# Reordering TensorE's instruction stream at the last and at the first pair of chunks: four handed-over matmuls, and four quadrant matmuls

## The chip, the cores and the metric

The kernel runs on one core of a Trainium2 chip. The metric is the device time of one execution in microseconds, given as the median of three runs.

## The reference: what is computed

The input x has 1024 examples, each with 64 features of 16 elements. Three layers of a compressed interaction network follow. Each forms all products of a feature of x with a feature of the layer's own input, and maps them by a weight matrix:

```python
z = jnp.einsum('bfe,bge->bfge', x0, h)          # all products of two features
y = jnp.einsum('oc,bce->boe', Ws[i], z) + bs[i][None, :, None]
if split_half and i != n - 1:
    x_i, h = (y[:, :half, :], y[:, half:, :])   # half to the output, half to the next layer
...
pooled = jnp.sum(jnp.concatenate(xs, axis=1), axis=2)
return pooled @ fc_w.T + fc_b
```

Everything is in float32; the output is one number for each example.

## The kernel before, in words

**Chunks and tiles.** The batch is cut into 32 chunks of 32 examples, so that a chunk has 32 x 16 = 512 columns. The pairs of features are laid out as 16 tiles (4 groups j of 4 tiles i) of 128 rows. A product block `z` holds one group: 128 x 4 x 512. VectorE makes most blocks (`w_product`, line 633; `product`, line 241), GpSimd some. 14 blocks exist, and each goes back to a list when its last reader has been written (`take`, `used`).

**What TensorE accumulates.** Since the last layer is followed only by a sum and a dot product, the kernel folds its weights: from each chunk it needs a hidden layer (`w_all[..., 0:64]`, 64 rows) and a second linear map of the same products, called q (`w_all[..., 64:128]`, 64 rows). Their elementwise product, summed, together with a term from x (`x_v0x`, line 289), gives the output. Every matmul of this part writes 64 output rows, thus one half of the array's columns; the code alternates between an upper and a lower half of a bank, so that two matmuls can stand in the array together.

**Pairs.** From chunk 6 on, chunks are taken two at a time, a and b, in 13 pairs. Two chunks times two maps are a 2 x 2 block product, and a scheme of seven instead of eight products is used. Its names: X, T2, T3, T4, B21, B22 are blocks and their sums and differences; alpha, beta, gamma, delta are accumulators in PSUM (`alpha` and `gamma` are the two row halves of one bank, `delta` and `beta` halves of two others). GpSimd makes the sums and differences (`w_mix`, line 650). One of them, the second group of T4 = T2 + B21, is made by an accumulating DMA that GpSimd issues (`nc.gpsimd.dma_start(..., accum_op=ALU.add)`, line 648).

**Order.** Nothing is scheduled automatically: `at(when, ...)` notes an operation with a place number, `zipped` notes two columns of matmuls that interleave, and all operations are then sorted by that number and issued. Per pair, `window` puts out two columns of matmuls: X with wq, T2 with s2, T3 with s1 to alpha in the first column; T3 with s3 and T2 with the hidden weights to delta, and T-blocks to beta, in the second. Four of the delta matmuls, those that read the T4 block made by DMA (`p4_run(p)[-LATE:]`), are left out there and handed over to the next pair's window, where they stand in the two `fill` lists (`first_fill`, `second_fill`); the eight B22 matmuls go there too (`late_run`). All matmuls of this part share line 525.

**Quadrant matmuls.** `squares` (placed at t + 30.2 in each window) issues four 64 x 64 matmuls that add squares of x and form y; they take one quadrant of the array each. VectorE's end-of-pair operations follow (`end_pair`): `w_hb` (line 671), `w_qa` (line 675), `w_uu` for alpha (line 681), `w_ha` (line 678), `w_uu` for delta (line 681), `x_v0x` (line 289), `sums` (line 293).

**The end.** The 13th pair has no window after it. Its handed-over work is zipped with the q matmuls of chunks 2 and 3 (`end_q`, first 384 columns, then 128), whose hidden layer is known from the start. `end_squares` issues their four quadrant matmuls and ends in line 929 and two ScalarE copies (931); `end_gamma` adds gamma to alpha (ScalarE 941, VectorE 942). `add_parts` (950), `end_uu` (935), pooling matmuls and output DMAs close the kernel.

Of the kernel before, what the change touches and what calls it, by code (L numbers as in the profile page):

```python
# [50 lines left out]
NI = 4  # L51
NJ = 4
NT = NI * NJ
# [11 lines left out]
GROUPS = [(j, i) for j in range(2) for i in range(NI)]  # L65
LATE = 4
# [3 lines left out]
def cin_kernel(ctx, tc, xra, xrb, wh, w0r, w1h, w2t, wx1, wx0, vec, out):  # L70
# [297 lines left out]
    for h in range(2):  # L368
        at = slice(32 * h, 32 * h + 32)
# [145 lines left out]
    def at(when, fn, *args, **flags):  # L515
        ops.append((when, len(ops), fn, args, flags))

    def zipped(when, *columns):
        for n, column in enumerate(columns):
            for m, job in enumerate(column):  # L520
                if job is not None:
                    at(when + m + n / len(columns), *job)
# [37 lines left out]
    def q_extra(c, w, out=None):  # L560
        out = accs[c][halves[1 - c % 2]] if out is None else out[halves[c % 2]]
        mm(out, w, es[c])
# [59 lines left out]
    def w_run(p, out, w, name, start=False, at_t=0, order=GROUPS):  # L622
        return [
            (w_job, p, out, w, j * NI + i + at_t, name, start and n == 0)
            for n, (j, i) in enumerate(order)
        ]
# [58 lines left out]
    def make_pair(t, p, when, mixed):  # L685
        a, b = p["a"], p["b"]
        for when, c, j, name, uses in (
            (when[0], b, 2, "B22", 5), (when[1], b, 0, None, 0), (when[2], b, 0, "T3", 9),
            (when[3], a, 0, "X", 5), (when[4], b, 3, "B22", 5), (when[5], b, 1, None, 0),
            (when[6], b, 1, "T3", 9), (when[7], a, 1, "X", 13 if p["k"] > 3 else 5), (when[8], a, 2, "B21", 5),  # L690
            (when[9], a, 3, "B21", 5),
        ):
            if name is None:
                at(t + when, w_both, p, j)
                continue
            if name == "B21" and j == 2 and p["k"] == 3:
                at(t + when, w_product, p, c, j, name, uses, engine=nc.gpsimd)
                continue
            if name != "T3":
                ahead = 3.3 if p["k"] > 4 and name == "B22" and j == 2 else 2.7  # L700
                if p["k"] == 3 and name == "X" and j == 1:
                    ahead = 9.1
                at(t + when - ahead, second, c, j)
            at(t + when, w_product, p, c, j, name, uses)
        t2, t1, t4 = ("T2", "X", "T3"), ("T3", "B22", "T2"), ("T2", "T2", "B21")
        for when, j, names in zip(
            mixed, (0, 1, 1, 0, 1, 1, 0), (t2, (*t2, 0, 2), (*t2, 2), t1, t1, t4, t4)
        ):
            at(t + when, w_mix, p, j, *names)
        at(t + 29, lambda: used(p["B21"][1]))  # L710

    def p4_run(p):
        return w_run(p, delta, wh_all, "T2", at_t=2 * NI)

    def first_fill(p):
        return [(lambda: q_extra(p["a"], va, p["beta"]),)] + p4_run(p)[-LATE : -LATE // 2]

    def second_fill(p):
        return p4_run(p)[-LATE // 2 :]

    def late_run(p, out=alpha, first=0, last=2 * NI):
        jobs = w_run(p, out, s4, "B22", out is gamma)[first:last]
        return jobs if last < 2 * NI else jobs + [(lambda: q_extra(p["b"], vb, p["alpha"]),)]
# [5 lines left out]
        v0x(b, "set")  # L729
        v0x(a, "set")  # L730

    def window(t, p, fill, late, pad=[], order=GROUPS[NI:] + GROUPS[:NI]):
        zipped(
            t,
            w_run(p, alpha, wq_all, "X", True, order=order) + fill[0] + w_run(p, alpha, s2, "T2")
            + fill[1] + w_run(p, alpha, s1, "T3"),
            w_run(p, delta, s3, "T3", True) + late + w_run(p, beta, wq_all, "B21", True, 2 * NI)
            + pad + p4_run(p)[:-LATE],
        )
        at(t + 30.2, squares, p)  # L740
        at(t + 7.3, snap_p1, p)
        at(t + 7.8, snap_p7, p)
        at(t + 7.3 + len(fill[0]) + 8, snap_u2, p)

    def end_pair(t, p, whens):
        hb_, qa, uub, ha, uua, xv, add = whens
        at(t + hb_, w_hb, p)
        at(t + qa, w_qa, p)
        at(t + uub, w_uu, p, alpha, "A", snaps[2])
        at(t + ha, w_ha, p)  # L750
        at(t + uua, w_uu, p, delta, "O", snaps[0])
        at(t + xv, x_v0x, p["k"])
        at(t + add, sums, p["k"])


    def load_pair(t, p, b0, a0, b1, a1):
        a, b = p["a"], p["b"]
        at(t + b0, load_xa, b)
        at(t + b0, load_xb, b, 2, 0)
        at(t + a0, load_xa, a)  # L760
        at(t + a0, load_xb, a, 0)
        at(t + b1, load_xb, b, 3, 1)
        at(t + a1, load_xb, a, 1, 2, 3)
        for c in (b, a):
            at(t + 1, load_e, c)
            at(t + 14, square, c)
        at(t + 1.1, load_xx, p["k"])
# [65 lines left out]
    for n in range(NPAIR):  # L833
        k = n + 3
        s = k % 2
        p = {
            "k": k, "A": halves[s], "O": halves[1 - s], "b": 2 * k + s, "a": 2 * k + 1 - s,
        }
        pairs.append(p)
        t = T0 + SPAN * n  # L840
        if n == 0:
            load_pair(t, p, -39.9, -33.3, -33.15, -27)
            make_pair(
                t, p, (-23.4, -20.7, -20.4, -17.8, -17.2, -16.8, -16.6, -7, -13.5, 3),
                (-14, -6.9, -6.8, 7.2, 12.4, 17.6, 17.5),
            )
            left5 = [[(contract_half, 5, 3, i, n) for i in (2, 3)] for n in range(2)]
            window(
                t, p, ([left5[1][0], (q_extra, 4, va)], [left5[1][1]]),
                [left5[0][0], (q_extra, 5, va), None, None], [left5[0][1], None],  # L850
                GROUPS,
            )
        else:
            q = pairs[-2]
            load_pair(t, p, -34, -28, -27.8, -27.7)
            make_pair(
                t, p, (-21.4, -18.7, -18.4, -15.8, -12.2, -9.5, -6.1, -2, 1.6, 4.2),
                (-5, 1.6, 3.6, 7.2, 12.4, 18.6, 18.5),
            )
            window(t, p, (first_fill(q), second_fill(q)), late_run(q))  # L860
            end_pair(t, q, (0.7, 11.7, 17.9, 22.3, 23.2, 24, 27.5))
# [40 lines left out]
    t, q = T0 + SPAN * NPAIR, pairs[-1]  # L902
# [64 lines left out]
        plain_product(t + when, c, j)  # L967
    for when, c in ((-5, 2), (0, 3)):
        at(t + when, product, c, NJ - 1, engine=nc.gpsimd, uses=NI)
    end_pair(t, q, (0.7, 4.5, 13.8, 8.5, 9, 9.5, 14.5))  # L970
    at(t + 10.5, end_gamma)
    at(t - 0.1, new_ends)
    zipped(
        t,
        first_fill(q) + second_fill(q) + late_run(q, gamma, 0, 2)
        + [(end_q, 3, m, 0) for m in range(NT)] + [(end_extra, 3, 0)],
        [(end_q, 2, m, 0) for m in range(3)] + late_run(q, first=2)
        + [(end_q, 2, m, 0) for m in range(3, NT)] + [(end_extra, 2, 0)],
    )
# [102 lines left out]
```

## Time and profile before

| | |
|---|---|
| median of 3 runs | 458.56 us (457.4 to 459.05) |
| the profiled execution | 458.11 us, of which the span from first to last instruction is 456.3 us |
| mean granted TensorE clock | 0.996 |
| TensorE matmul busy | 447.7 us (98%) |
| VectorE busy | 392.8 us (86%) |
| GpSimd busy | 364.4 us (80%) |
| ScalarE busy | 116.5 us (26%) |
| a 64-row, 512-column matmul record | 0.593 us mean, started 0.43 us apart |
| accumulating DMA z<-z, 1 MB, 13 of them | 8.6 / 9.5 / 12.3 us from issue to landing (least, median, longest) |

PE is TensorE's matmuls, PEld its weight loads, DVE VectorE, ACT ScalarE, POOL GpSimd, SP the engine on whose queue the loads from memory are issued. "A <-B" behind an idle time says what ended the wait. Times in the timeline count from the span's start. A matmul's record includes filling and draining, so that neighbours overlap: its cost is read from the distance of starts. One matmul of the code stands as two records.

### The profile page before, as it was taken

To read this page: it belongs to the slowest core of one execution; us is meant where nothing else is said; L and a number is where in the kernel's file an instruction comes from. 1 tells how busy PE (TensorE), PEld (TensorE's weight loads), DVE (VectorE), ACT (ScalarE), POOL (GpSimd) and SP (SyncE) were. 2 spreads that over 40 slices of the span, in tenths; PEclk is the share of its full clock that TensorE was granted. 3 is DMA by queue.
4 is the path that set the end of the run, shared out by engine and by line. 5 is a ranking of instruction groups with operands and counts; after the bars stand their busy time and mean duration, and the time that the engine had idled before them with its cause. 6 is when DMAs were issued, how large, how long until landed. Compare 5 with 4: busy or idle time off the path is not lost.

```text
span 456.3 us, 6069 instructions
## 1 busy us (share of the span) xinstructions
PE 447.7 (98%) x2302; PEld 161.6 (35%) x2302; DVE 392.8 (86%) x284; ACT 116.5 (26%) x215; POOL 364.4 (80%) x125
## 2 busy tenths in 40 slices
PE   8999999999999999999999999999999999999897
PEld 4565343332333333333333333333333333333235
DVE  4995499998989998989999998999999899998443
ACT  3162251232313113121312312231321313133011
POOL 5423688998997979799897979899797979979700
PEclk9999999999999999999999999999999999999899
DMA  8996998496839396784939587593949769571400
GB/s 304 408 306 151 315 407 338 138 317 194 286 82 344 106 268 228 172 323 103 354 87 293 190 208 290 117 381 65 312 149 253 256 136 386 111 232 23 105 0 2
DMA packets 34484, 99.67 MB, mean 218 GB/s; under 512 B 6324, under 2 KB 6996, under 8 KB 27864
## 3 DMA queue, kind: packets, MB, share of 16 engines
q1 hardware_dynamic: 31800, 84.70, 51.7%
q0 software_dynamic: 1872, 13.63, 16.6%
q10 hardware_dynamic: 784, 0.95, 0.8%
q8 instruction: 18, 0.29, 0.3%
q14 instruction: 10, 0.08, 0.0%
HBM read 84.00 MB, written 1.64 MB: 188 GB/s over the span
## 4 chain that ended last, share of the span: by engine, by line
PE 80%; DVE 10%; issue 4%; DMA 4%; POOL 1%; SPq 0%; ACT 0%; POOLq 0%; ACTq 0%
PE alpha L525 48%; PE delta L525 9%; PE acc L525 6%; PE acc L251 6%; DVE z L633 5%; PE q L525 3%; PE acc L269 3%; PE beta L525 3%; DMA z<-z 2%; DMA z<-in_w0r 2%; DVE acc L293 1%; POOL z L650 1%; DVE uu L289 1%; DVE uu L681 1%; DVE delta L678 1%
## 5 line engine op out<-in xcount | busy, mean ns | idle before, releaser
L650 POOL TENSOR_TENSOR z<-z,z 128x2048 f32<-128x2048 f32 (+1 forms) x78 | 299.8, 3876 | 29.6 <-PE alpha L525 29.6
L633 DVE TENSOR_TENSOR z<-xa,xp 128x2048 f32<-128x2048 f32 x103 | 231.6, 2279 | 1.2
L525 PE MATMUL alpha<-z,ws 128*64 128x512 f32 x624 | 219.5, 593 | 0.0
L525 PEld LDWEIGHTS alpha<-z,ws 128*64 128x64 f32 x624 | 69.4, 137 | 117.6 <-issue 117.6
L525 PE MATMUL delta<-z,w_all 128*64 128x512 f32 x208 | 97.2, 601 | 3.4 <-DMA z<-z 2.3
L553 ACT COPY xp<-xb 128x512 f32<-128x512 f32 x88 | 51.5, 587 | 167.0 <-DVE z L633 140.6
L525 PE MATMUL alpha<-z,w_all 128*64 128x512 f32 x208 | 92.0, 595 | 0.8
L525 PE MATMUL delta<-z,ws 128*64 128x512 f32 x208 | 92.0, 595 | 0.0
L525 PE MATMUL beta<-z,w_all 128*64 128x512 f32 x208 | 91.7, 593 | 0.0
L241 DVE TENSOR_TENSOR z<-xa,xp 128x2048 f32<-128x2048 f32 (+2 forms) x23 | 45.1, 2001 | 6.8 <-ACT xp L553 5.8
L525 PEld LDWEIGHTS alpha<-z,w_all 128*64 128x64 f32 x208 | 27.5, 137 | 63.6 <-issue 53.0
L241 POOL TENSOR_TENSOR z<-xa,xb 128x2048 f32<-128x2048 f32 x6 | 27.5, 4644 | 20.5 <-DMA xb<-in_xrb 20.5
L525 PEld LDWEIGHTS delta<-z,w_all 128*64 128x64 f32 x208 | 28.7, 139 | 36.0 <-issue 30.3
L251 PE MATMUL acc<-z,w_all 128*64 128x256 f32 x256 | 29.0, 382 | 1.1 <-DVE z L241 0.9
L525 PE MATMUL acc<-z,w_all 128*64 128x512 f32 (+1 forms) x96 | 29.4, 594 | 0.0
L525 PEld LDWEIGHTS beta<-z,w_all 128*64 128x64 f32 x208 | 27.9, 137 | 0.0
L525 PEld LDWEIGHTS delta<-z,ws 128*64 128x64 f32 x208 | 27.5, 137 | 0.1
L664 ACT ACTIVATE snap<-alpha,vs 64x512 f32<-64x512 f32 x13 | 8.9, 682 | 54.3 <-PE alpha L525 54.3
L251 PEld LDWEIGHTS acc<-z,w_all 128*64 128x64 f32 x256 | 18.0, 137 | 13.3 <-DVE z L241 2.5
L661 ACT COPY snap<-alpha 64x512 f32<-64x512 f32 x13 | 7.6, 581 | 48.8 <-PE delta L525 48.8
L293 DVE TENSOR_REDUCE acc<-uu 128x64 f32<-128x1024 f32 (+2 forms) x19 | 19.6, 1036 | 0.2
L681 DVE SCALAR_TENSOR_TENSOR uu<-alpha,snap 64x512 f32<-64x512 f32 x13 | 9.0, 689 | 12.1 <-PE alpha L525 12.1
(117 smaller groups left out, 361.1 us busy)
## 6 DMA issues: line engine op xcount, KB each, us to landing
xa<-in_xra SPq DMA_DIRECT2D x32, 1024.0 KB, 9.7
xb<-in_xrb SPq DMA_DIRECT2D x128, 256.0 KB, 7.8
z<-z POOLq DMA_DIRECT2D x13, 1024.0 KB, 9.5
e<-in_xra SPq DMA_DIRECT2D x28, 128.0 KB, 6.8
xx<-in_xra SPq DMA_DIRECT2D x28, 128.0 KB, 5.7
z<-in_w2t SPq DMA_DIRECT2D x2, 1024.0 KB
z<-in_wx SPq DMA_DIRECT2D x2, 1024.0 KB, 9.4
z<-in_w1h SPq DMA_DIRECT2D x1, 1024.0 KB
```

Of the source, the lines that this page charges most:

```text
L241: engine.tensor_tensor(blocks[zs[c, j]][:, at, :], xas[c][:, at, :], xbs[c][j].unsqueeze(1).to_broadcast([128, last - first, N]), ALU.mult,)
L251: nc.tensor.matmul(accs[c][halves[n]], w_all[:, t, 0:64], blocks[zs[c, j]][:, i, n * H2 : (n + 1) * H2], start=(t == 0), stop=(j == last a ...
L269: nc.tensor.matmul(accs[c][halves[1 - c % 2]], w_all[:, t, 64:128], blocks[zs[c, j]][:, i, :], start=(t == 0), stop=False, skip_group_chec ...
L289: nc.vector.scalar_tensor_tensor(uu[:, to, :], ys[k], cx, xxs[k], ALU.add, ALU.mult)
L293: nc.vector.tensor_reduce(acc[rows, of, k, half], uu[rows, of if at is None else at, E * half.start : E * half.stop].rearrange("p k (b e) ...
L525: nc.tensor.matmul(out, w, rhs, start=start, stop=stop, skip_group_check=True)
L553: nc.scalar.copy(bank, xbs[c][j])
L633: engine.tensor_tensor(blocks[b], xas[c], xbs[c][j].unsqueeze(1).to_broadcast([128, NI, N]), ALU.mult)
L650: nc.gpsimd.tensor_tensor(*(blocks[b][:, first:last] for b in (o, x, y)), ALU.subtract if in1 == "T3" else ALU.add,)
L661: nc.scalar.copy(snaps[0][p["O"]], alpha(p))
L664: nc.scalar.activation(snaps[1][p["O"]], alpha(p), AF.Identity, bias=bh1[p["A"]])
L681: nc.vector.scalar_tensor_tensor(uu[p[out], 0], x(p), 1.0 / QS, factor[p[out]], ALU.mult, ALU.mult)
```

## The change

In the last pair the four handed-over delta matmuls, which stood right after the beta matmul in the first column, are put behind gamma's two matmuls and the first six q matmuls of chunk 3. VectorE's `w_ha` and its `w_uu` go from places 8.5 and 9 to 13.3 and 13.5. In the first pair's window `squares` goes from t + 30.2 to t + 21.9, ahead of the last T3 matmul of group 0, the four of group 1, and the four delta matmuls that interleave with those.

```diff
-    def window(t, p, fill, late, pad=[], order=GROUPS[NI:] + GROUPS[:NI]):
+    def window(t, p, fill, late, pad=[], order=GROUPS[NI:] + GROUPS[:NI], quads=30.2):
...
-        at(t + 30.2, squares, p)
+        at(t + quads, squares, p)
...
                 [left5[0][0], (q_extra, 5, va), None, None], [left5[0][1], None],
-                GROUPS,
+                GROUPS, 21.9,
...
-    end_pair(t, q, (0.7, 4.5, 13.8, 8.5, 9, 9.5, 14.5))
+    end_pair(t, q, (0.7, 4.5, 13.8, 13.3, 13.5, 9.5, 14.5))
...
     zipped(
         t,
-        first_fill(q) + second_fill(q) + late_run(q, gamma, 0, 2)
-        + [(end_q, 3, m, 0) for m in range(NT)] + [(end_extra, 3, 0)],
+        first_fill(q)[:1] + late_run(q, gamma, 0, 2) + [(end_q, 3, m, 0) for m in range(6)]
+        + p4_run(q)[-LATE:] + [(end_q, 3, m, 0) for m in range(6, NT)] + [(end_extra, 3, 0)],
         [(end_q, 2, m, 0) for m in range(3)] + late_run(q, first=2)
         + [(end_q, 2, m, 0) for m in range(3, NT)] + [(end_extra, 2, 0)],
     )
```

The second column is as before. The order on GpSimd and on SP's queue is the same in both kernels.

## The prediction

> **What bounds the kernel now.** The page comes first: engine shares and slices.
>
> ```profile
> PE 447.7 (98%) x2302; PEld 161.6 (35%) x2302; DVE 392.8 (86%) x284; ACT 116.5 (26%) x215; POOL 364.4 (80%) x125
> PE   8999999999999999999999999999999999999897
> PEclk9999999999999999999999999999999999999899
> ```
>
> TensorE is busy nearly everywhere; so only a place where it stands idle, or runs slowly, has time to give. The slices show one: PE and its clock dip to 8 in slice 38 (from 422 us). The chain in order of time says what ends there.
>
> ```profile
> 416.50 0.50 POOL z L650
> 417.08 1.14 issue
> 418.26 1.87 issue
> 420.13 9.17 DMA z<-z
> 429.34 0.91 PE delta L525
> ...
> 438.49 0.57 PE hx L525
> 439.51 11.14 PE q L525 x90
> ```
>
> The chain leaves TensorE for an accumulating DMA (z<-z, issued on POOL's queue at L648) and comes back at 429.34. From there to the end it is TensorE again. The timeline of that place (start, duration, instruction, idle before it):
>
> ```profile
> 429.34 1.11 PE L525 MATMUL delta<-z,w_all 128*64 128x512 f32 x1 [2.27 <-DMA z<-z]
> 430.24 1.06 PE L525 MATMUL delta<-z,w_all 128*64 128x512 f32 x1
> 431.10 1.06 PE L525 MATMUL delta<-z,w_all 128*64 128x512 f32 x1
> ...
> 432.74 0.59 PE L525 MATMUL delta<-z,w_all 128*64 128x512 f32 x1
> 433.17 0.59 PE L525 MATMUL delta<-z,w_all 128*64 128x512 f32 x1
> ```
>
> Read the starts: 0.86 to 0.90 apart at first, 0.43 later. Each matmul of the code stands in the trace as two records, so one 512-column matmul costs 0.86 us warm and 1.7 in this slow stretch; one of 384 columns costs 0.64 (records 0.32 apart). Stage windows (last columns: granted clock, DMA share, GB/s) confirm it:
>
> ```profile
> 427.00:432.70 5.70, 3.43 (x10) 1.65 (x11) 0.68 (x1) 0.00 (x0) 3.05 (x1) 0.70 0.05 15
> 432.70:438.40 5.70, 5.70 (x29) 2.03 (x25) 2.03 (x3) 0.00 (x0) 0.00 (x0) 1.00 0.00 0
> ```
>
> The first pair's end, from the timeline, has the change's other place:
>
> ```profile
> 107.06 0.64 PE L525 MATMUL delta<-z,w_all 128*64 128x512 f32 x1 [1.11 <-POOL z L650]
> 110.64 0.64 PE L525 MATMUL alpha<-e,vs 64*64 64x512 f32 x1
> 111.66 0.64 PE L525 MATMUL alpha<-z,w_all 128*64 128x512 f32 x1
> 111.75 0.76 DVE L671 SCALAR_TENSOR_TENSOR snap<-alpha,vs,snap 64x512 f32<-64x512 f32 x1 [1.84 <-PE y L525]
> 119.31 0.13 PEld L525 LDWEIGHTS delta<-z,w_all 128*64 128x64 f32 x1 [0.59 <-DMA z<-z]
> 119.43 0.59 PE L525 MATMUL delta<-z,w_all 128*64 128x512 f32 x1
> ```
>
> TensorE idles 1.11 for POOL's last difference; the quadrant matmuls (64x64) stand behind it, 1.02 us with their drains. The line to remember is 119.31: the next pair's handed-over matmuls need that pair's DMA, and their weight load already waits 0.59 for it. The DMA was issued at 106.92 and took 12.3 us, the longest of the 13 (median 9.5); DMA share there is about 1.
>
> **What the Trainium skill says.** "TensorE: Matmul & The Clock Gate", Part 1: an idle TensorE falls to half clock, judged over free-running windows of about 3.4 us. The trace agrees: half speed after an idle of 2.27, none after 1.11. Where between these the threshold lies depends, by that page, on the window's phase. "TensorEngine Tiling (Array Packing)", Key Properties: tiles execute independently; a change of tiling mode drains the array. The trace agrees: an alpha matmul begins at 431.96, ahead of a delta (432.74) that precedes it in program order but goes to the other column half; and there is about 0.1 us at each side of quadrant matmuls.
>
> **Part 1, the last pair.** Removed: nothing. Moved: four delta matmuls from steps 1 to 4 of the first column to steps 9 to 12, behind two gamma and six of chunk 3's q. POOL's and SP's orders stay, so DMA issue times do too.
> Gone: the idle from about 426.9, when the next matmul could have begun, to 429.34 (2.44), and the slow stretch: four deltas took 429.34 to 434.46, 5.12 instead of 4 x 0.86 = 3.43, so 1.69. By 432.5, when the new order reaches delta, the DMA has been there for three microseconds; the first column has had beta, two gammas and six q, 0.86 + 1.72 + 3.86, since 426.0.
> Added: the order counts by column half, since the two run side by side. Up to the quadrants: the second half has 3 q (1.93) and 7 of 512 columns (6.02), 7.95; the first now has 7.30. Gamma's first matmul is now at step 1 and carries a wait on DVE in the built order: it overwrites a part of alpha's bank that L671 has just read. L671 runs from 426.08 to 426.84, and beta occupies the array to 426.9; I charge 0.25 for wait and restart, with the second q behind it. Quadrants at 426.0 + 7.95 + 0.25 + 0.1 = 434.3, done at 435.35 (1.02). After them the first half has 3 deltas (2.58) and 11 q (7.08) and sets the pace: 445.0. In the trace before the 384-column q end at 448.5. **Sum: -3.5.** If the halves went in lockstep, each mixed step at 0.86, it would be 0.5 less (13 x 0.86 + 11 x 0.64 against 17.0 by columns, less what the second half already holds): -3.0.
> DVE: L678 and its L681 move behind L289, L929 and L942. Nothing waits for them but the sums. Had they stayed, L289 would stand behind the late delta, and the second y bank's reuse with it. Chain: delta's last at about 438.2, L942 ends at 438.8 (hx 435.4, L929 0.7, three ACT copies 1.8, L942 0.7), then L678 0.7, two L681 1.4, sums 1.2, L289 0.75, sums 0.7, L950 0.7: 444.4, ahead of the 445.2 at which L935 wants DVE. Cover: 0.8 us; beyond that the end is late one for one.
> After 445 the 128-column q, pooling and output follow unchanged.
>
> **Part 2, the first pair.** The quadrants go between the third and fourth T3 matmul of the first half, 104.9. Third ends at 104.92, quadrants to 106.04, fourth to 106.9: all in front of POOL's end at 106.99. The four differences then start at 107.06 as before, and the next pair at 110.55 instead of 111.66: 1.11 gained. Its DVE input ends at 109.91, in time; L671 loses its 1.84 wait, so DVE runs 1.8 early. But the next thing is the DMA: the delta behind beta is reached at 118.3 instead of 119.4, its data land at 119.31. TensorE stops for 1.0 and goes on at 119.43, as before. **Sum: 0.** Idle time moves from 106 to 118. Worse is possible: DVE's early products release SP's next chunk load at about 115.3 instead of 117.05, and it competes with the accumulation for its last 2 us. Accumulating beside little other traffic took 9.2 us, in contention 12.3; so up to 2 x (1 - 9.2/12.3) = 0.5 is lost. I take +0.1.
> The later pairs keep their rhythm of 26.1 to 26.3 us, since every long wait in them (POOL and ACT on alpha, DVE on alpha) is on TensorE. Their accumulations have slack: 131.86 + 9.5 = 141.4, used at about 145.5.
>
> **Sum against the profile.** The profiled execution took 458.11 (span 456.3), 0.45 below the median of 458.56; the change is a difference, so -3.4 from the median: **455.1**.
>
> **Rivals.**
> *Part 2's gain is kept.* If the accumulation came about 1 us sooner, the 1.0 would be carried to the end: -4.5, 454.1. For: later pairs saw 9.5 us. Against: neither its issue nor its traffic moves to the better. Chance 0.10.
> *It lands later, or the new stop at 118.3 cools the clock.* A stop of 1.5 lies between 1.11 (stayed warm) and 2.27 (did not). Up to 0.5, and 1.7 more if cold: 455.6 to 457.3. Chance 0.16.
> *DVE's tail.* If L678's chain is over 0.8 late, L935 and the pools wait; losing 1 to 2: 456 to 457. For: delta is its last input. Against: the sum above. Chance 0.07.
> *Slower: unequal matmuls don't run side by side.* The place is the first-column steps with a q against a 512-column matmul, 12 now where there were 6. Were each pair serial (1.50), the stretch takes 12 x 1.50 + 0.86 + 11 x 0.64 + 1.1 = 27.0 from 426.0: 453.0, 4.5 later than before: 463. It turns slower once a mixed step costs about 0.3 above 0.86. Against: at 436 to 438 q and alpha records overlap at 0.32 and 0.43. Chance 0.04.
> *The change doesn't do what it says.* The built order has the matmuls where the diff puts them, with their waits; only a cold clock at the end for another reason would leave 457. Chance 0.03.
>
> **How the numbers follow.** My forecast (0.60) has 454.7 to 455.6. The range 453.8 to 456.9 takes in the kept gain, the later landing and most of DVE's tail. About 0.5%, 2.3 us, is what a measurement of this kernel can tell from no change, so faster means below 456.3: the forecast, the kept gain, and most of the late landings, 0.84; same 0.12 (cold clock, tail, no effect); slower 0.04.
>
> **What would show it.** Right: no DMA wait of PE between 424 and 446; clock 1.00 there; the first gamma at 426.9; L678 behind L942. In the first pair: no gap ahead of the quadrants at 105, next pair at 110.5, and a new PE wait on DMA z<-z of about 1 us at 118.3. Wrong: no such wait (the gain was kept), q records 0.43 apart beside alpha, or L935 held by DVE's own queue.

## The result, and the profile after

Over seven runs each, the kernel after took 453.6 us in the median (453.13 to 454.65), the kernel before 458.16 (455.37 to 459.05): a ratio of 0.991, 95% interval 0.9886 to 0.9935. The forecast was 455.1, with a range from 453.8; the median lies 0.2 below its low end. The forecast was counted from the 458.56 of three runs; on that scale the ratio of 0.991 gives 454.4. The profiled execution took 453.26 us, span 451.4, clock 1.000, against 458.11, 456.3 and 0.996.

The page of the kernel after, engine shares and slices:

```profile
PE 446.7 (99%) x2302; PEld 162.4 (36%) x2302; DVE 392.8 (87%) x284; ACT 116.6 (26%) x215; POOL 364.7 (81%) x125
PE   8999999999999999999999999999999999999997
```

The dip in slice 38 is gone. The chain in order of time (start, length, what) of the same kernel no longer goes through a DMA at the end:

```profile
423.60 0.57 PE alpha L525
424.62 0.47 PE beta L525
426.96 0.43 PE alpha L525 x2
431.25 0.43 PE delta L525
431.69 0.43 PE delta L525
432.11 0.86 PE alpha L525 x3
432.97 0.57 PE hx L525
433.99 0.47 PE delta L525
436.71 9.06 PE q L525 x76
```

From beta to the last q matmuls it is TensorE alone. The timeline of the last pair on TensorE (start, duration, instruction, idle before it in brackets where there is one):

```profile
424.55 0.64 PE L525 MATMUL beta<-e,va 128*64 128x512 f32 x1
425.03 0.59 PE L525 MATMUL beta<-e,va 128*64 128x512 f32 x1
425.46 0.64 PE L525 MATMUL alpha<-z,ws 128*64 128x512 f32 x1
...
431.09 0.59 PE L525 MATMUL delta<-z,w_all 128*64 128x512 f32 x1
431.52 0.59 PE L525 MATMUL delta<-z,w_all 128*64 128x512 f32 x1
...
432.91 0.64 PE L525 MATMUL y<-e,v 64*64 64x512 f32 x1
...
433.92 0.64 PE L525 MATMUL delta<-z,w_all 128*64 128x512 f32 x1
...
443.64 2.13 PE L525 MATMUL q<-z,w_all 128*64 128x128 f32 x32
```

No bracket, and 0.43 us from start to start. The stage windows (length, then busy time of PE, PEld, DVE, ACT, POOL, then clock, DMA share, GB/s) confirm full clock in the 11 us in which the kernel before idled and ran slowly:

```profile
426.70:432.40 5.70, 5.70 (x31) 2.87 (x27) 0.30 (x1) 0.00 (x0) 1.95 (x1) 1.00 0.01 3
432.40:438.10 5.70, 5.70 (x34) 2.45 (x34) 2.06 (x3) 1.81 (x3) 0.00 (x0) 1.00 0.00 0
```

From beta's start to the start of the first 128-column q that follows the last 384-column one it takes 443.64 - 424.55 = 19.09 us; before, 448.52 - 425.99 = 22.53. So the last pair gave 3.44 of the 4.9 by which the spans differ.

The other 1.44 is the earlier start of beta, and the first pair shows where it comes from. TensorE and its weight loads in the kernel after:

```profile
103.75 1.02 PE L525 MATMUL alpha<-z,ws 128*64 128x512 f32 x2
104.70 0.64 PE L525 MATMUL alpha<-e,vs 64*64 64x512 f32 x1
...
105.72 0.64 PE L525 MATMUL alpha<-z,ws 128*64 128x512 f32 x1
105.72 0.64 PE L525 MATMUL delta<-z,w_all 128*64 128x512 f32 x1
...
109.21 0.59 PE L525 MATMUL alpha<-z,w_all 128*64 128x512 f32 x1
...
110.06 0.59 PE L525 MATMUL delta<-z,ws 128*64 128x512 f32 x1
```

```profile
117.94 0.13 PEld L525 LDWEIGHTS delta<-z,w_all 128*64 128x64 f32 x1 [0.88 <-DMA z<-z]
```

The quadrants stand where the prediction put them, the wait for GpSimd is gone, and the weight load of the handed-over delta now waits 0.88 for the accumulating DMA. But that DMA was issued earlier than before. GpSimd's timeline, first of the kernel after, then of the kernel before:

```profile
69.04 4.56 POOL L536 TENSOR_TENSOR z<-z,vs 128x2048 f32<-128x2048 f32 x1 [1.65 <-DMA z<-in_wx]
105.50 0.98 POOL L648 DMA_DIRECT2D z<-z  x1
```

```profile
70.67 9.13 POOL L536 TENSOR_TENSOR z<-z,vs 128x2048 f32<-128x2048 f32 x2 [2.47 <-DMA z<-in_wx]
106.92 0.96 POOL L648 DMA_DIRECT2D z<-z  x1
```

GpSimd's chain begins with the landing of two weight blocks (`in_wx`, L536) and then runs without a long wait to L648. In this execution it started 1.63 earlier there, at a place where the two programs are the same, and reached L648 1.42 earlier. The experiments ask whether this belongs to the change.

### The profile page after: what moved, and what is told of

The parts are those of the page before. It is cut to its first block, busy times and chain, and to the rows that moved or that the text cites. A ratio compares the mean times of both kernels' runs of the same rounds, so it can differ in the third digit from the quotient of the medians.

```text
span 451.4 us, 6068 instructions
## 1 busy us (share of the span) xinstructions
PE 446.7 (99%) x2302; PEld 162.4 (36%) x2302; DVE 392.8 (87%) x284; ACT 116.6 (26%) x215; POOL 364.7 (81%) x125
## 4 chain that ended last, share of the span: by engine, by line
PE 84%; DVE 10%; issue 3%; DMA 1%; SPq 0%; ACT 0%; ACTq 0%
PE alpha L525 51%; PE delta L525 10%; PE acc L525 7%; PE acc L251 6%; DVE z L633 5%; PE q L525 3%; PE acc L269 3%; PE beta L525 3%; DMA z<-in_w0r 1%; DVE acc L293 1%; DVE uu L289 1%; DVE uu L681 1%; DVE delta L678 1%; DVE xp L639 1%; PE y L525 0%
## 5 line engine op out<-in xcount | busy, mean ns | idle before, releaser
L650 POOL TENSOR_TENSOR z<-z,z 128x2048 f32<-128x2048 f32 (+1 forms) x78 | 300.0, 3881 | 29.5 <-PE alpha L525 29.3
L525 PE MATMUL delta<-z,w_all 128*64 128x512 f32 x208 | 95.8, 593 | 0.0
L525 PE MATMUL q<-z,w_all 128*64 128x384 f32 (+1 forms) x128 | 20.0, 382 | 0.0
```

Source lines behind the costliest of these rows:

```text
L525: nc.tensor.matmul(out, w, rhs, start=start, stop=stop, skip_group_check=True)
L650: nc.gpsimd.tensor_tensor(*(blocks[b][:, first:last] for b in (o, x, y)), ALU.subtract if in1 == "T3" else ALU.add,)
```

## The experiments

Theory A: the last pair gives all, and the first pair nothing, since the accumulating DMA lands some 12.4 us after its issue and TensorE meets it. Rival B: the first pair's gain is kept, and with it the other 1.4 us. Rival C: the moved quadrants make the DMA land later, or cool the clock. All the runs with this DMA in its place can be set side by side once GpSimd's arrival is taken out: the table's last column is the profiled execution's time less the issue of the first pair's L648.

| kernel | ratio to before, interval | profiled time | L648 issued | beta starts | beta less L648 | beta to 128-column q | time less L648 |
|---|---|---|---|---|---|---|---|
| before | | 458.11 | 106.92 | 425.99 | 319.07 | 22.5 | 351.2 |
| before, again | 1.0015, 0.9995 to 1.0034 | 457.78 | 106.48 | 425.63 | 319.15 | 22.5 | 351.3 |
| first pair only | 1.0001, 0.9979 to 1.0022 | 456.54 | 106.89 | 425.87 | 318.98 | 21.1 | 349.7 |
| last pair only | 0.9928, 0.9903 to 0.9953 | 454.30 | 106.54 | 425.61 | 319.07 | 19.1 | 347.8 |
| after | 0.991, 0.9886 to 0.9935 | 453.26 | 105.50 | 424.55 | 319.05 | 19.1 | 347.8 |
| after, again | 0.9924, 0.9901 to 0.9947 | 454.13 | 106.51 | 425.52 | 319.01 | 19.1 | 347.6 |
| after, third | 0.9933, 0.9913 to 0.9954 | 454.36 | 106.77 | 425.67 | 318.90 | 19.1 | 347.6 |
| gamma only | 0.9952, 0.9935 to 0.9969 | 455.86 | 107.66 | 426.72 | 319.06 | 19.6 | 348.2 |

**The kernel before once more** (no edit), on one chip with the three that follow:

> The kernel before, unchanged, for a second trace. Theory A (GpSimd's arrival): how early the first pair's accumulating DMA is issued varies between executions with the landing of the in_wx loads, so its issue lies anywhere between 105 and 107 us, and the delta matmul of the next pair starts 12.4 us after the issue or at its own reach of about 118.3 to 119.4, whichever is later. Rival B (the change moves it): the kernel before always issues it at about 106.9, and 119.4 follows. Ratio 1.000 for both; the last pair's idle of 2.0 to 2.5 us before the first delta and slow matmuls behind it.

Measured: 458.02 us, ratio 1.0015 (0.9995 to 1.0034). The trace has the same stop for the DMA, 2.23 us, and from about a microsecond behind it the records stand 0.86 apart. L648 was issued at 106.48, and the next pair's delta waited for its landing at 119.02, which is theory A's picture. Over all comparisons the runs of this one program reach from 455.35 to 459.73: 4 us, as much as the change is worth.

**The first pair alone:**

```diff
-    def window(t, p, fill, late, pad=[], order=GROUPS[NI:] + GROUPS[:NI]):
+    def window(t, p, fill, late, pad=[], order=GROUPS[NI:] + GROUPS[:NI], quads=30.2):
...
-        at(t + 30.2, squares, p)
+        at(t + quads, squares, p)
...
-                GROUPS,
+                GROUPS, 21.9,
```

> Only the first pair's quadrant matmuls moved. Theory A (the next DMA wait takes the gain): 0 to -0.4 us, ratio 0.999 to 1.000; the next pair starts 1.1 us sooner behind GpSimd's last difference, and its first delta waits for the DMA and starts 12.4 us after the DMA's issue. Rival B (the gain is kept): -1.1 us, ratio 0.9976.

Measured: 457.58 us, ratio 1.0001 (0.9979 to 1.0022). TensorE's timeline of this kernel, first pair and the next window:

```profile
107.00 0.64 PE L525 MATMUL delta<-z,w_all 128*64 128x512 f32 x1
...
110.55 0.59 PE L525 MATMUL delta<-z,ws 128*64 128x512 f32 x1
...
119.26 0.64 PE L525 MATMUL delta<-z,w_all 128*64 128x512 f32 x1 [0.82 <-DMA z<-z]
119.27 0.64 PE L525 MATMUL alpha<-z,ws 128*64 128x512 f32 x1
```

The wait of 1.11 ahead of the last difference is gone and the next pair begins at 110.55 instead of 111.66; at 119.26 both halves stand for the DMA, issued at 106.89. Beta starts at 425.87, as before. This is theory A's picture; rival B falls for this part, and the DMA's 12.37 us speak against C: SP's next load did come 1.0 earlier (116.05 instead of 117.05), and the landing stayed. The end of the same timeline holds a surprise:

```profile
429.40 0.64 PE L525 MATMUL delta<-z,w_all 128*64 128x512 f32 x1 [2.45 <-DMA z<-z]
429.88 0.59 PE L525 MATMUL delta<-z,w_all 128*64 128x512 f32 x1
```

The old order's stop is here too, longer than the 2.27 of before, yet the next records stand 0.43 apart: the clock did not fall, and the stretch took 21.1 instead of 22.5.

**The last pair alone** (the change without the argument 21.9):

> Only the last pair's order changed. Theory A: -3.4 us, ratio 0.9925; from the beta matmul to the end of the 384-column q it takes 19.1 us where the kernel before takes 22.5. Rival B: -3.4 as well. Rival C (the last pair is worth more in most executions than in the profiled one, since the slow stretch is longer there): -4.5, ratio 0.990.

Measured: 454.31 us (453.46 to 455.45), ratio 0.9928 (0.9903 to 0.9953). In the first pair the last difference was awaited 0.21 by PE, and the next window's weight load 0.66 for the DMA, landing 12.46 after its issue. By the medians this kernel is 2.7 us below the kernel before, where 3.4 was expected, and by the traces 3.4; rival C's 4.5 is out. The gain that can be told apart is all in this kernel.

**The kernel after once more** (no edit):

> The changed kernel, unchanged, for a second trace and beside its parts. Theory A: -3.4 to -3.8, like part 2 alone within 0.4 us. Rival B: -4.5, 1.1 beyond part 2 alone. Rival C: -4.5, equal to part 2 alone.

Measured: 454.05 us (453.68 to 455.51), ratio 0.9924 (0.9901 to 0.9947). Beside the last pair alone, on the same chip, moving the quadrants as well brings nothing that can be told apart. L648 is at 106.51 and in_wx's wait 2.40, near the kernels of the old order: 1.0 of the 1.4 by which the first profile's GpSimd was early was that execution's. For the rest a doubt stays. In the seven traces of kernels with both parts of the change L536 starts at 68.95 to 70.10, in the six others at 70.25 to 71.41. No reason was found why edits that come later in the program should act there, and on this chip the medians of the two kernels are 0.3 apart; a small effect is not excluded.

**No accumulating DMA at the first and last pair, before and after.** If the landing eats the first pair's gain, the gain must appear when there is nothing to land. In both kernels, in `w_mix`:

```diff
         if in1 == "B21" and j:
+            if p["k"] in (3, NPAIR + 2):
+                return
             nc.gpsimd.dma_start(out=blocks[o], in_=blocks[y], accum_op=ALU.add)
```

> The kernel before, with the accumulating DMA left out in the first and in the last pair (those two T4 blocks lack their second addend). Theory A (the landing is the bound at both places): first pair: nothing gained, since TensorE's own reach of the next delta (12.4 us after GpSimd's last difference ends) is about the landing; last pair: no idle and no slow stretch, from the beta matmul to the end of the 384-column q 18.1 us instead of 21.1 to 22.5. Ratio 0.990 to 0.993. Rival B (something else than the DMA stands ahead of the last deltas): 21 or more remain.

> The changed kernel, with the accumulating DMA left out in the first and in the last pair (those two T4 blocks lack their second addend). Theory A: the first pair's gain is no longer taken by the landing, so the next pair's first delta starts 11.3 us after GpSimd's last difference ends, where it took 12.4; last pair as in the changed kernel, 19.1 us. Ratio to the kernel before 0.988 to 0.991, about equal to the kernel before without these DMAs (-1.1 + 1.0). Rival B (GpSimd or VectorE take the gain as well): 12.4 again, and 1 us slower than the kernel before without these DMAs.

Measured: 454.39 us, ratio 0.9938 (0.9918 to 0.9958), and 453.71, ratio 0.9927 (0.9912 to 0.9942); both ratios lie above what was expected, and the intervals overlap, so the traces decide. From the last difference's start to the next window's first handed-over delta: 107.94 to 120.32 = 12.4 us with the old place of the quadrants, 106.72 to 117.92 = 11.2 with the new one, and no wait for a DMA in either. So the gain is there when the landing is taken away: A. But it is not kept whole. Beta starts 318.93 us after the last difference in the one (426.87 - 107.94) and 318.43 in the other (425.15 - 106.72): 0.5 of the 1.2 arrives. TensorE's timeline of the kernel with the quadrants moved and no DMA says why:

```profile
106.54 0.64 PE L525 MATMUL alpha<-z,ws 128*64 128x512 f32 x1
106.72 0.64 PE L525 MATMUL delta<-z,w_all 128*64 128x512 f32 x1
...
110.20 0.59 PE L525 MATMUL alpha<-z,w_all 128*64 128x512 f32 x1
...
110.89 0.59 PE L525 MATMUL delta<-z,ws 128*64 128x512 f32 x1
```

Read it by halves of the array. Behind the quadrants one half has five T3 matmuls to alpha, the other four differences to delta. With GpSimd so early that the differences hardly wait, there is no gap for the fifth: the half with four goes over to the next pair's X at 110.20, the one with five to its delta at 110.89. The lag is still there seven microseconds later (beta 117.07 in the one, alpha 117.75 in the other), and the lagging half sets the pace: it is 1.72 ahead of the same matmul in the other kernel (119.47), and beta at the end is 1.72 ahead too, of which 1.22 is the earlier difference. Counted from that difference, the second kernel's profiled time is 0.4 longer (453.84 - 106.72 = 347.1 against 454.64 - 107.94 = 346.7): the first pair brings 0.5, and the last pair costs 0.9.

The 0.9 is seen at the end. The first of the two kernels gives a floor for it: with the old order and data that are there, beta to the 128-column q takes 18.19 us (426.87 to 445.06). The new order takes 19.09 even without a DMA to wait for; it costs 0.9 against an old order that never waits. The two traces show where. From beta to the quadrants it is 8.35 us against 8.09, from there on 10.74 against 10.10. The 0.26 ahead of the quadrants is the term for gamma's wait: the third q record starts 0.90 after the first (424.56 to 425.46 in the kernel after), against 0.69 in the old order without a DMA (426.88 to 427.57), and the next record is 0.05 later still. The 0.64 behind them is the unequal halves: 3 deltas and 11 q in one (9.6 by the costs above) beside 14 q in the other (9.0), where the old order has 14 q in both.

**The two quadrant blocks of the end made one**, to take back some of that 0.9. To the kernel after:

```diff
-    def end_squares():
-        hx = ps.tile([128, N], F32, tag="set", name="hx")
+    hxs = []
+
+    def end_quads():
+        hxs.append(ps.tile([128, N], F32, tag="y", name="hx"))
         for c in (2, 3):
-            h_extra(c, hx, True)
-            v0x(c, "set")
+            h_extra(c, hxs[0], True)
+            v0x(c, "y")
+
+    def end_squares():
+        hx = hxs[0]
...
-        at(t, square, n)
+        at(t - 3, square, n)
...
+    at(t - 0.75, end_quads)
     at(t + 9.9, end_squares)
```

> The changed kernel, with the last four quadrant matmuls (chunks 2 and 3) put directly behind the pair's own, their two results in the y banks, and their squares on ScalarE three places earlier; VectorE's use of them stays where it was. The barrier between the two column halves falls away. Theory A (halves run side by side, each at its own rate): from the first quadrant matmul to the end of the 384-column q 19.1 us instead of 20.1 (each half has 7 x 0.86 + 17 x 0.64 = 17.0, two sets of quadrants 1.9, 0.25 for the wait), so -0.9 us against the changed kernel. Rival D (mixed steps go in lockstep): -0.2 us, only the two drains.

Measured: 453.79 us (452.71 to 454.77), ratio 0.9933 (0.9916 to 0.9949), without the kernel after on the same chip. From the start of the last pair's quadrants to the 128-column q: 424.11 to 443.18 = 19.07 us, against 423.53 to 443.64 = 20.11 in the kernel after; that is theory A's size, and rival D's 0.2 is out. The profiled time less L648 is 452.71 - 106.24 = 346.5, 1.1 to 1.3 under the kernels after.

**The DMA issued ahead of the difference that TensorE awaits**, on top of that; if the landing is what binds the first pair, an earlier issue should free it:

```diff
-                (-14, -6.9, -6.8, 7.2, 12.4, 17.6, 17.5),
+                (-14, -6.9, -6.8, 7.2, 12.4, 17.4, 17.5),
```

> As the kernel before it in this list, and in the first pair GpSimd issues the accumulating DMA ahead of its last difference instead of behind it. Theory A: the DMA is issued 4.5 us sooner and lands in time, the last difference ends 0.8 us later and TensorE waits for it about 0.8; the next pair's first delta then starts at its own reach, about 12.1 us after the old issue time instead of 12.4: -0.3 us more. Rival: the landing was not the bound, and the later difference costs 0.8: +0.8.

Measured: 454.19 us (452.48 to 455.24), ratio 0.9936 (0.9916 to 0.9955): no gain over the merged quadrants alone. GpSimd's timeline, then TensorE's:

```profile
101.94 1.01 POOL L648 DMA_DIRECT2D z<-z  x1 [1.15 <-DVE xp L639]
102.70 9.44 POOL L650 TENSOR_TENSOR z<-z,z 128x2048 f32<-128x2048 f32 x2
```

```profile
107.56 0.64 PE L525 MATMUL delta<-z,w_all 128*64 128x512 f32 x1 [0.66 <-POOL z L650]
```

The wait for the DMA near 118 is gone, as meant, but the issue itself waited 1.15 on GpSimd's queue, the difference behind it came later by that and by the issue's own time, and TensorE waits for it again. One wait took the other's place, and at a loss that the early GpSimd of this execution hides: counted from the first L650 behind L536, the profiled time is 452.90 - 78.02 = 374.9, against 373.7 and 373.8 in the two traces of the merged quadrants (79.03 and 79.34). The 1.1 to 1.2 lost is about the wait of 1.15; -0.3 was expected, and 0.8 by the rival. The trace names L639 on VectorE as what L648 waited for; why was not settled.

The same run shows that the 12.4 us of the other traces are no fixed length. The time to landing of all 13 transfers of L648, first in the kernel before, then in this one:

```profile
DMA to landing us min/median/max: 8.6/9.5/12.3
```

```profile
DMA to landing us min/median/max: 8.4/9.5/9.8
```

In the kernel before the longest is the first pair's, issued at 106.92 among seven loads on SP's queue (issued from 105.45 to 108.8). Issued at 101.94, 1.8 ahead of the first of these loads, the same transfer landed within 9.8 us. That the loads make the difference was not tested apart from the time of issue.

**Gamma alone ahead of the four deltas**, to price the parts of the new order. To the kernel before:

```diff
-        first_fill(q) + second_fill(q) + late_run(q, gamma, 0, 2)
+        first_fill(q)[:1] + late_run(q, gamma, 0, 2) + p4_run(q)[-LATE:]
         + [(end_q, 3, m, 0) for m in range(NT)] + [(end_extra, 3, 0)],
```

> The kernel before, with the last pair's four delta matmuls put behind gamma's two alone, and no q of chunk 3 ahead of them; first pair and VectorE's order as before. Theory A: TensorE reaches the delta 2.6 us after the beta matmul's start and waits some 0.7 us for the DMA, too little for the clock to drop, so clock 1.00 in every execution; from the beta matmul to the end of the 384-column q 19.4 us, against 22.5 (slow stretch) or 21.1 (none) before and 19.1 in the changed kernel. Ratio 0.993 to 0.995, and a scatter of the times of 2 us as in the changed kernel, not of 4. Rival: any wait for the DMA brings the slow stretch, 20.5 or more.

Measured: 455.06 us (454.15 to 457.01, 17 runs), ratio 0.9952 (0.9935 to 0.9969). TensorE's timeline:

```profile
430.01 0.64 PE L525 MATMUL delta<-z,w_all 128*64 128x512 f32 x1 [0.46 <-DMA z<-z]
```

Two gammas leave 0.46 of the wait, and in this execution the clock stays. "Clock 1.00 in every execution" did not hold: 3 of the 17 runs have a mean granted clock of 0.996, in no trace that would show where, and the times scatter over 2.9 us, not 2. For the kernel after it is 1 of the 24 runs measured. Beta to the 128-column q takes 426.72 to 446.27 = 19.55: of the 3.44 two matmuls bring 2.98, and the order with the six q 0.46 more.

**The kernel after a third time**, and **the merged quadrants again**, side by side on one chip:

> The changed kernel again, on the same chip as the next one. 19.1 us from the beta matmul to the end of the 384-column q; ratio 0.992 to 0.994 by theory A.

> The kernel with the quadrant matmuls merged, again, beside the changed kernel. If its end is worth what its trace showed, 1.0 us (0.2%) below the changed kernel; if another wait takes it, equal.

Measured: 454.49 us (453.46 to 455.53), ratio 0.9933 (0.9913 to 0.9954), and 453.0 (452.14 to 454.03), ratio 0.990 (0.9868 to 0.9931). The trace of the second has the quadrants at 424.47 and the 128-column q at 443.53, 19.06 us, as in the first trace of that kernel. It is the best of these kernels: 1.5 us ahead of the kernel after by these medians and 1.0 by the stretch, though the two intervals overlap.

## Why the prediction was right, and where its sizes were off

**Part 1, -3.5.** Right, within 0.1: 3.44 by the traces. Its times hold too, all earlier by the 1.44 by which beta starts earlier: gamma predicted at 426.9, found at 425.46 (+1.44 = 426.90); quadrants 434.3, found 432.91 (434.35), with 0.26 for gamma's wait where 0.25 was charged; end of the 384-column q 445.0, found 443.64 (445.08). The halves did not go in lockstep, so -3.5 and not -3.0, and the rival of serial mixed steps (463) falls: records of 512 columns stand 0.43 apart in one half beside 384-column ones 0.32 apart in the other. This agrees with what the prediction took from the Trainium skill's "TensorEngine Tiling (Array Packing)", Key Properties, that tiles execute independently.

**VectorE's tail.** Right in size. The timeline of VectorE after:

```profile
436.70 0.71 DVE L942 TENSOR_TENSOR alpha<-alpha,snap 64x512 f32<-64x512 f32 x1 [1.91 <-ACT snap L941]
437.44 0.69 DVE L678 TENSOR_TENSOR delta<-delta,snap 64x512 f32<-64x512 f32 x1
...
442.24 0.71 DVE L950 TENSOR_TENSOR acc<-acc 128x32 f32<-128x32 f32 x2
443.86 0.56 DVE L935 SCALAR_TENSOR_TENSOR uu<-q,snap 128x384 f32<-128x384 f32 x1 [0.91 <-PE q L525]
```

L678 is behind L942, L950 ends at 442.95, and L935 then waits 0.91 for TensorE: the cover of 0.8 that was worked out. That L289 would hold up the end if L678 had stayed was argued and not tried.

**Part 2, 0.** Right in its sum and in its mechanism when GpSimd arrives as in the trace of before: with the first pair alone, the next pair at 110.55 and the stop at 119.26, against 110.55 and 119.43 in the prediction. The charge of 0.1 for a later landing was too much: from issue to landing it took 12.2 to 12.5 us in ten traces with this DMA in its old place, before and after alike. Nor did the new stop near 118 cool the clock, by 23 of the 24 runs of the kernel after, which have 1.000; so rival C has nothing to stand on. One step holds for that arrival only: "1.11 gained". With the first pair alone both halves of the array have it (110.48 and 110.55); with GpSimd earlier it is the gain of one half. The fourth T3 matmul was said to end "in front of POOL's end"; with GpSimd 1.4 earlier it doesn't, as the trace after shows (one half goes over at 109.21, the other at 110.06). Without a DMA at all 0.5 of it was on offer, by the two kernels without it, so the rival at 454.1, which kept all of it, was too generous also.

**The sum, -3.4 from 458.56.** Here lies the miss of 1.5 us. The median of the three runs was 0.4 above that of seven. The rest is the difference of the medians, -4.56 there, and it did not come back: in two later comparisons it is 454.05 - 457.05 = -3.0 and 454.49 - 457.48 = -3.0. Both medians of the first comparison lie on the side that makes the distance large: the kernel before at 458.16 against 457.05 and 457.48 later, the kernel after at 453.6 against 454.05 and 454.49. The ratio of 0.991 is thus in part the luck of a few runs drawn from a kernel that scatters over 4 us. The scatter of single executions has two terms that the prediction took as fixed.

- GpSimd's arrival: L648 was issued between 105.50 and 107.66 in ten traces, and in the eight of the table beta follows it by 318.9 to 319.2, whichever parts of the change are in. That is the 1.44 of the profiles shown first. L648 itself follows the end of GpSimd's wait for in_wx (69.04 after, 70.67 before) by 36.2 to 36.9, most where GpSimd waits for the second of the two blocks as well (0.65 in the third trace of the kernel after); what makes that landing earlier or later was not tested.
- The slow stretch of 1.69: it was there in two of three traces with the old order's stop, and not in the third. The mean granted clock of single runs is on record and counts it: in these three traces 0.996 goes with one slow stretch, and 1.000 with none. Of 77 runs of the kernel before, 33 have 1.000, 34 have 0.996 and 10 have 0.993. On the chip of the first four experiments the runs with 1.000 have a median of 455.71 (12 runs), those with 0.996 of 458.07 (13), beside 454.05 for the kernel after; on the chip of the last three 456.80 and 457.89, beside 454.49. So part 1 is worth 3.4 by the traces where the clock fell (351.2 to 347.8 in the last column) and 2.0 where it didn't (349.7 to 347.8); by these medians 3.4 to 4.0, and 1.7 to 2.3. The mean of this fits -3.0 (estimated from the stretches and the counts: 1.99 + 1.45 x 44/77 = 2.8, or 3.0 if 0.993 stands for two slow stretches, which no trace shows).

On the clock the prediction said that the trace agrees with the skill's "TensorE: Matmul & The Clock Gate", Part 1. It does so in part only. That page has the clock fall after at least one idle window of about 3.4 us; here stops of 2.27 and 2.23 were enough, and the measurement decides. The page also says that the windows run freely; if so, the same stop can go either way, as 2.45 without a fall beside 2.27 with one does. The windows themselves are in no trace.

So the forecast's -3.4 was for the profiled execution and right for it. Set against a median it should have been nearer -3.0, since 33 of 77 executions keep the full clock and lose no slow stretch.

## What to carry to other kernels

Where TensorE stops for a transfer, move ahead of it only as much other work as the stop is long, and count by array half: two matmuls brought 3.0 of the 3.4 us here. Before filling a wait for an engine, ask what else that engine has under way that the filling doesn't make earlier: here its DMA, which landed 12.4 us after its issue, gave the same stop a few microseconds on. Compare such kernels from an event that both share (here that issue): runs of one program differed by 4 us, while the time counted from the issue repeated within 0.2 wherever the clock did the same.

## What the runs showed of the hardware that was not expected

- A stop of 2.45 us left TensorE's clock at full speed in one execution; 2.27 and 2.23 halved it in two others, in one of these only about a microsecond after TensorE had gone on (the kernel before, again). Of 77 runs of this order 44 have a mean clock below 1.000.
- The 1 MB accumulating DMA at the first pair took 12.2 to 12.5 us in ten traces, though issued up to 2.2 us apart and with different work on VectorE beside it. Issued some 4 us earlier, ahead of seven loads instead of among them, it took 9.8; the median of the 13 in the kernel after is 9.4.
- The two halves of the array kept a lag of 0.69 us over seven microseconds of matmuls, without one waiting for the other. Behind the quadrants of the last pair, the longer half's own sum of matmuls (9.66 us in the prediction) was the length: 9.72, which is 10.74 less the quadrants' 1.02.
